# A graph layer and a parallel LSTM on one core: additions moved from GpSimd to VectorE, the state comparison moved three steps ahead, stores on two queues, zeros and the fc weight in other shapes

## Chip, core and metric

The kernel runs on one core of a Trainium2 chip. The metric is the device time of one execution in microseconds (us); the kernel before takes 1112.99 us, the median of three runs (1111.95, 1112.99 and 1113.43). A core has five instruction queues, each in order: TensorE (PE; PEld are its weight loads), VectorE (DVE), ScalarE (ACT), GpSimd (POOL) and SyncE (SP). SP, ACT and POOL also issue DMA transfers.

## The reference, cut to what matters

```python
x = x + gnn(layernorm(x), src, dst, ...)       # 1250 nodes of 512 features, 20000 edges
x = x + lstm(layernorm(x))                     # one sequence of 1250 steps, hidden size 512

def gnn(feat, src, dst, ...):
    h = feat @ fc_w.T + fc_b
    norm = clip(segment_sum(1, dst), 1) ** -0.5
    res = layer(h, h, w1_1, w2_1, b_1, 1)
    return layer(res, h, w1_2, w2_2, b_2, 2)   # layer: sum over edges, two 512x512 products, bias, relu

def step(h_prev, c_prev, x_t):                 # combined = [x_t, h_prev]
    f, i, o = (sigmoid(combined @ W + b) for W, b in three gates)
    c = f * c_prev + i * tanh(combined @ W_c + b_c)
    h = o * tanh(c)                            # h is the output of the step
```

## The kernel before

**Rows.** The 1250 rows are cut into 32 stretches (`P`) of 40 rows (`LEN`). A tile of 128 partitions holds four rows of each stretch, and ten tiles (`T`) hold all rows.

**Start.** In the block that opens the pools `prep`, `edges` and `psT`, SP and ACT issue the loads in the order of the code: edge lists (L292), the last rows of x (L134, on ACT), tile 0 of x (L120), the weight `fcw` as one transfer of 1 MB (L300), tiles 1 to 3 (L120), the bias `fcb`, tiles 4 to 9 (L126), then `w2`, two biases and the zeros. There are eight counters for the transfers of SP and ACT, used in turn: a transfer that takes a counter again waits until the transfer eight places before it has landed. GpSimd makes `ident`, the numbers `ids_f` and a block of zeros in `planes` (L320, 12 partitions of 6144 elements), which SP writes to ten DRAM tensors (L322).

VectorE turns the edge lists into numbers of tiles and stretches (`neg_floor_div`), takes the layer norm's statistics of the tiles (`stats`, `scales`), and compares for the one-hot matrices (`make_onehot`, L401 and L403). TensorE transposes `fcw` (`turn_fcw`, L377: for each of four blocks of columns, four transposes of 128x128), multiplies the tiles (`product`, L176) and adds up the adjacency counts (`count_group`, L417). The order in which PE, DVE and ACT take this work is the order of the code, written by hand in the loop over `s`, for `T + 3` slots.

**Middle.** After two graph layers (L750) the input part of the gates is multiplied for the LSTM (L919) and written to the DRAM tensors `xp_d`, from which each step fetches its 96 rows.

**LSTM.** The 32 stretches run side by side, 40 steps (n = 0 to 39) after 96 steps of warm-up from zero state: 12 in a short form, 84 as full steps (n = -84 to -1). A step is a chain in two halves `s`: matmuls with the state (L604, `add_gates`), three activations (L611, L613, L615), product and sum (L617, L618), tanh (L620), the output `hh` (L621) and its transpose `hT` (L622), which the next step's matmuls wait for. From n = 0 on, GpSimd adds `hh` to the row buffer `x2c` (L1032); after n = 7, 15, 23, 31, 37 and 39 the finished rows are stored (`store`, L831). All stores are issued by SP but the last, which goes over SP, ACT and POOL.

**Comparison.** The warm-up is right where a stretch's state at n = 0 is the state that the stretch before it has after its step 39. `keep_state` (L890, L891) copies states at n = 0 and after the loop; then four DVE instructions (L1039 to L1043), a matmul (L1045) and a conversion (L1047) count the places that are further apart than `TOL` = 2^-18. Every engine loads this count (L1048); if it is above zero, all 1250 steps are run again in order (L1050 ff.), else the branch goes to the end of the program (L1110), where all engines meet.

Of the kernel before, what the change touches and what calls it, by code (L numbers as in the profile page):

```python
# [38 lines left out]
def gnn_lstm_kernel(  # L39
# [118 lines left out]
        nc.vector.tensor_scalar(ve, mv[:, :, 1], EPS, None, OP.add)  # L158
        rsqrt(pool, ve, out, name)

    def transpose_in(ps, rows):

        p = ps.tile([128, KD, R], F32, name="psT")
        for k in range(KD):
            nc.tensor.transpose(p[:, k, :], rows[:, k * 128:(k + 1) * 128], ident)
        return p
# [37 lines left out]
    with ExitStack() as gnn_stack:  # L204
# [77 lines left out]
        with tc.tile_pool(name="prep", bufs=1) as prep, \  # L282
# [14 lines left out]
            load_last_rows(xt, nc.scalar, fill=True)  # L297
            load_rows(0, 1, xt)
            fcw = prep.tile([128, KD, D], F32, name="fcw")
            nc.sync.dma_start(fcw, fc_w.rearrange("(a p) i -> p a i", p=128))  # L300
            biases = [prep.tile([R, D], F32, name=name) for name in ("fcb", "b1", "b2")]
            fcb, *bl = biases
            load_rows(1, 4, xt)
# [12 lines left out]
            nc.gpsimd.iota(ids_f, pattern=[[1, widest]], base=0, channel_multiplier=0,  # L316
                           allow_small_or_imprecise_dtypes=True)

            zeros = planes.rearrange("b t i d -> b (t i d)")[:4 * EARLY, :12 * G]
            nc.gpsimd.memset(zeros, 0.0)  # L320
            for v in xp_d:
                nc.sync.dma_start(  # L322
                    bass.AP(tensor=v.tensor, offset=v.offset,
                            ap=[[12 * G, 4 * EARLY], [1, 12 * G]]), zeros)

            with tc.manual_schedule(engines={mybir.EngineType.PE, mybir.EngineType.DVE,
                                             mybir.EngineType.Activation}):
# [9 lines left out]
                def scales(t0, t1):  # L337
                    layernorm_scale(prep, mv[:, t0:t1, :], rstd[:, t0:t1], f"ln{t0}")
                    nc.vector.scalar_tensor_tensor(nmr[:, t0:t1], mv[:, t0:t1, 0], -1.0,
                                                   rstd[:, t0:t1], op0=OP.mult, op1=OP.mult)  # L340


                ends = []
                for name, rows in rows_i:
# [7 lines left out]
                    nc.vector.tensor_copy(e, p[:ER, 0:2, :EC // 2])  # L352
                    ends.append(e.rearrange("p i c -> p (i c)"))
                e_src, e_dst = ends
                none = edges.tile([ER, BW * T], F16, name="none")
                nc.vector.memset(none, 0.0)
                ids = edges.tile([ER, widest], F16, name="ids")
# [14 lines left out]
                fcT = prep.tile([128, KD, D], F32, name="fcT")  # L372

                def turn_fcw(k):
                    p = psM.tile([128, D], F32, name="psM")
                    for a in range(KD):
                        nc.tensor.transpose(p[:, a * 128:(a + 1) * 128],  # L377
                                            fcw[:, a, k * 128:(k + 1) * 128], ident)
                    nc.scalar.copy(fcT[:, k, :], p)

                turn_fcw(0)
                turn_fcw(1)
                np_src, o_src = neg_floor_div(e_src, LEN, "stretch")
                stats(0, 1)
                scales(0, 1)
                turn_fcw(2)
                na_src, q_src = neg_floor_div(o_src, 4, "tile")
                nc.vector.scalar_tensor_tensor(low, np_src, -4.0, q_src, op0=OP.mult, op1=OP.add)
                nc.vector.scalar_tensor_tensor(key, e_dst, float(T), na_src,
# [31 lines left out]
                            done.append((blocks.pop(i), i))  # L421
                    return done

                xns, xTs, hTs, ps_h, ps_b = {}, {}, {}, {}, {}

                def normed(t):
                    if t < T:
                        xns[t] = work.tile([R, D], F32, name="xn")
                        nc.scalar.activation(xns[t], xt[:, t, :], AF.Identity,
                                             bias=nmr[:, t:t + 1], scale=rstd[:, t:t + 1])  # L430

                BATCH = 4
                n_batch = EC // BATCH
                counted = 0
# [30 lines left out]
                for s in range(T + 3):  # L465
                    c0, c1, c2 = per_slot[s] if s < len(per_slot) else (0, 0, 0)
                    if 0 < s < 3:

                        ps_h[s - 1] = product(psM, xTs.pop(s - 1), fcT)
                        count(c0)  # L470
                    if s < T:
# [12 lines left out]
                    count(c1)  # L484
                    if 0 <= s - 2 < T:
                        hTs[s - 2] = transposed(prep2, psT, h[:, s - 2, :], "hT")
                    if 0 <= s - 1 < T:
                        nc.vector.tensor_add(h[:, s - 1, :], ps_h.pop(s - 1), fcb)
                    count(c2)
                    if s == 2:  # L490
                        for l in range(2):
                            with_identity(w2[l], ALPHA * betas[l], ALPHA * (1.0 - betas[l]))
                    if 0 <= s - 3 < T:


                        hT = hTs.pop(s - 3)
                        ps, name = (psM, "psM") if s < T + 1 else (acc, "acc")
                        if s == T + 1:
                            total(psT.tile([128, KD, R], F32, name="psT")[:1, 0, :1])
                            split_first(prep2, order[3:7])  # L500
                        if s == T + 2:
                            add_base(T - 2)
                            split_first(prep2, order[7:9])
                        ps_b[s - 3] = [product(ps, hT, w2[0], name)]
                        if s == T:
                            most_edges()
                            count_edges(psT.tile([128, KD, R], F32, name="psT")[:, 0, :])
# [351 lines left out]
        def lstm(first_yT, Wx, bx, Wh, wh_parts, close_wx):  # L859
# [4 lines left out]

            TOL = 2.0 ** -18
# [7 lines left out]
            with ExitStack() as pools:  # L875
# [8 lines left out]
                held = S.rearrange("b i r -> b (i r)")[:, :3 * 256].rearrange(  # L884
                    "b (n x y) -> b n x y", n=3, x=8)
                snap, last, apart = held[:, 0], held[:, 1], held[:, 2, :, :31]

                def keep_state(dst, hT):
                    for s in range(2):
# [86 lines left out]
                with tc.manual_schedule(engines={mybir.EngineType.PE, mybir.EngineType.DVE,  # L976
# [32 lines left out]
                    fetch_wanted()  # L1009
                    for n in range(-WARM, LEN):  # L1010
                        u = AHEAD + WARM + n
                        if n == 0:
                            keep_state(snap, hT)
                        if u == len(units):
                            load_x2c()
                        xs = steps.pop(0)
# [11 lines left out]
                            cell(cells, ps[s], cgs[s], s, hh, hT[s])  # L1028
                        if u < len(units):
                            put(u, 2)  # L1030
                        if n >= 0:
                            nc.gpsimd.tensor_add(x2c[:, n, :], x2c[:, n, :], hh)  # L1032
# [7 lines left out]
                nc.vector.scalar_tensor_tensor(apart, apart, -1.0, apart, op0=OP.mult, op1=OP.max)  # L1040
                nc.vector.tensor_scalar(apart, apart, TOL, None, OP.is_le)
                near = seq.tile([128, 1], F32, name="near")
                nc.vector.tensor_reduce(near, apart, mybir.AxisListType.XY, OP.add)  # L1043
                pc = ps_c.tile([R, G], F32, name="pc")[:1, :1]
                nc.tensor.matmul(pc, near, ones, start=True, stop=True)  # L1045
                far = seq.tile([1, 1], I32, name="far")
                nc.vector.tensor_scalar(far, pc, -1.0, float(128 * 8 * 31), OP.mult, OP.add)  # L1047
# [67 lines left out]
```

## Time and profile before

| | us |
|---|---|
| Median of three runs | 1112.99 |
| The profiled execution | 1113.26 |
| Its span, first to last instruction | 1111.5 |
| Start, before TensorE is filled | 0 to 36 |
| Rest of the edge counting and first products | 36 to 195 |
| Graph layers, gate inputs, short warm-up | 195 to 485 |
| Full warm-up steps, n = -84 to -1 | 485 to about 918 |
| Steps n = 0 to 39 | to 1100.6 |
| After the last step | 1100.6 to 1111.5 |

In a timeline a row gives the start, the duration, the engine, the line of the code, the operation, output and inputs, and in brackets how long the engine stood idle before the row and what ended that. A queue's name with a q (POOLq, SPq) marks work of the sequencer alone, such as a DMA issue, a branch or a drain; it is not counted as busy. Tiles that were placed in another's memory show that one's name: `adj` in the LSTM is `sg`, `pr`, `th` or `hh`, `S` holds the kept states, `base` is x at the start and `x2c` in the LSTM.

### The profile page before, as it was taken

Reading aid. Unit: us, or ns where it says so; the run is one execution under the profiler, and the core shown is the slowest. Engines: PE = TensorE matmul, PEld = TensorE weight load, DVE = VectorE, ACT = ScalarE, POOL = GpSimd, SP = SyncE. Lnnn points to the kernel's source line nnn. Section 1 sums busy time; section 2 is a strip of 40 time slices with the busy share of each in tenths; the row PEclk is TensorE's granted clock in tenths of the full one; section 3 lists DMA queues with packets and bytes.
Section 4 is the critical chain, followed back from the end, with each engine's and each line's share of the span. In section 5 each row is a group of like instructions: output and inputs, shape, how many; then the busy total and the mean of one; then the engine's idle time right before and its main releaser. Section 6 shows DMA issues by size and latency. Waiting matters only on the chain.

```text
span 1111.5 us, 26611 instructions
## 1 busy us (share of the span) xinstructions
PE 1007.0 (91%) x10972; PEld 517.7 (47%) x10972; DVE 516.4 (46%) x1753; ACT 342.8 (31%) x1267; POOL 81.9 (7%) x138
## 2 busy tenths in 40 slices
PE   4899999999999998999999988888888888888884
PEld 2455454554455443344444444444444444444442
DVE  7767667102400665655544544444444444444443
ACT  2322125203401024443333333333333333333332
POOL 2000000100000011111001170000000000011001
PEclk9899999999999999999999999999999999999998
DMA  7500000600200037662323393332233333334431
GB/s 217 79 1 1 1 1 35 234 1 18 74 1 1 0 113 230 205 184 82 109 85 114 101 231 97 97 90 87 88 89 99 88 88 87 107 77 116 119 78 20
DMA packets 37271, 98.51 MB, mean 89 GB/s; under 512 B 5711, under 2 KB 10680, under 8 KB 37018
## 3 DMA queue, kind: packets, MB, share of 16 engines
q1 hardware_dynamic: 27280, 68.67, 23.1%
q0 software_dynamic: 7232, 23.63, 6.2%
q10 hardware_dynamic: 2625, 4.39, 1.3%
q8 instruction: 89, 1.46, 0.5%
q14 instruction: 45, 0.36, 0.1%
HBM read 74.29 MB, written 19.76 MB: 85 GB/s over the span
## 4 chain that ended last, share of the span: by engine, by line
PE 49%; issue 26%; DVE 13%; ACT 7%; DMA 1%; SPq 1%; POOL 1%; DVEq 0%; ACTq 0%; POOLq 0%
PE gates L604 29%; PE psM L919 8%; PE psM L176 8%; DVE adj L617 3%; ACT adj L620 3%; DVE hT L622 2%; DVE cg L618 2%; DVE adj L621 2%; ACT cg L611 2%; PE acc L417 2%; ACT adj L613 2%; DVE od L403 1%; DMA fcw<-in_L_gnn_fc_w_dram 1%; POOL xp_d L939 1%; PE gates L596 1%
## 5 line engine op out<-in xcount | busy, mean ns | idle before, releaser
L604 PE MATMUL gates<-Wh,hT 128*32 128x256 f32 x7936 | 457.5, 381 | 61.4 <-DVE hT L622 61.3
L604 PEld LDWEIGHTS gates<-Wh,hT 128*32 128x32 f32 x7936 | 233.4, 109 | 257.1 <-DVE hT L622 122.9
L617 DVE TENSOR_TENSOR adj<-adj,cg 128x128 f32<-128x128 f32 x248 | 68.2, 275 | 231.7 <-ACT adj L613 231.5
L919 PE MATMUL psM<-Wx,xT 128*128 128x512 f32 x320 | 147.6, 607 | 0.5 <-DVE adj L929 0.5
L750 PE MATMUL agg<-adj,planes 128*128 128x512 bf16 x720 | 130.1, 344 | 1.9 <-DVE x L463 1.9
L611 ACT ACTIVATE cg<-gates 128x64 f32<-128x64 f32 x248 | 55.4, 224 | 213.6 <-PE gates L604 210.1
L620 ACT ACTIVATE adj<-cg 128x64 f32<-128x64 f32 x248 | 63.6, 256 | 131.7 <-DVE cg L618 131.7
L750 PEld LDWEIGHTS <-planes 128*128 128x128 bf16 x720 | 70.4, 98 | 62.4 <-DVE x L463 2.7
L621 DVE TENSOR_TENSOR adj<-adj 128x64 f32<-128x64 f32 x248 | 55.9, 225 | 82.5 <-ACT adj L620 82.5
L919 PEld LDWEIGHTS psM<-Wx,xT 128*128 128x128 f32 x320 | 58.7, 192 | 71.3 <-issue 69.0
L622 DVE STREAM_TRANSPOSE hT<-adj 128x64 f32<-128x64 f32 x248 | 60.9, 245 | 24.2 <-DVE adj L621 1.4
L613 ACT ACTIVATE adj<-gates 128x128 f32<-128x128 f32 x248 | 67.2, 271 | 0.1
L618 DVE TENSOR_TENSOR cg<-adj 128x64 f32<-128x64 f32 x248 | 55.8, 225 | 8.5
L939 POOL DMA_DIRECT2D xp_d<-planes x40 | 28.8, 719 | 408.4 <-issue 214.2
L176 PE MATMUL psM<-w,hT 128*128 128x512 f32 x128 | 58.6, 610 | 0.0
L615 ACT ACTIVATE adj<-gates 128x64 f32<-128x64 f32 x248 | 57.0, 230 | 0.0
L403 DVE TENSOR_SCALAR od<-ids,key 125x820 f16<-125x820 f16 (+42 forms) x160 | 55.6, 347 | 0.0
L596 PE MATMUL gates<-h,sel 96*32 96x256 bf16 x992 | 50.0, 273 | 0.0
L1032 POOL TENSOR_TENSOR base<-base,adj 128x128 f32<-128x128 f32 x40 | 18.4, 459 | 414.9 <-DVE adj L621 414.9
L417 PE MATMUL acc<-od,ob 125*128 125x400 f16 (+22 forms) x360 | 46.4, 259 | 0.4
L401 DVE TENSOR_SCALAR ob<-ids,low 125x128 f16<-125x128 f16 x160 | 39.6, 247 | 15.5 <-PE acc L417 15.4
L931 ACT CAST planes<-adj 128x512 bf16<-128x512 f32 x40 | 24.7, 618 | 60.8 <-DVE adj L929 60.7
(163 smaller groups left out, 722.3 us busy)
## 6 DMA issues: line engine op xcount, KB each, us to landing
h<-xp_d SPq DMA_DIRECT2D x136, 384.0 KB
xp_d<-planes POOLq DMA_DIRECT2D x40, 384.0 KB, 3.1
base<-x POOLq DMA_DIRECT2D x40, 64.0 KB, 4.5
w<-in_L_gnn_w_dram SPq DMA_DIRECT2D x2, 1024.0 KB
w<-in_L_gnn_w_dram POOLq DMA_DIRECT2D x2, 1024.0 KB, 5.9
xp_d<-planes SPq DMA_DIRECT2D x10, 144.0 KB
h<-in_x_dram SPq DMA_DIRECT2D x10, 128.0 KB
h<-in_x_dram SPq DMA_DIRECT2D x10, 120.0 KB
```

Of the source, the lines that this page charges most:

```text
L176: nc.tensor.matmul(p, lT[:, k, :], rhs[:, k, :], start=(k == 0), stop=(k == KD - 1))
L417: nc.tensor.matmul(blocks[i][:, (d0 - i * BW) * T:(d1 - i * BW) * T], ob, od[:, (d0 - lo) * T:(d1 - lo) * T], start=False, stop=last)
L604: nc.tensor.matmul(ps[s][32 * j:32 * (j + 1), :, :], hT[b // 2][:, b % 2, :], Wh[:, b, :, 128 * j + 64 * s:128 * j + 64 * (s + 1)], start= ...
L611: nc.scalar.activation(cg[:, 1, :], p[:, 3, :], AF.Tanh)
L613: nc.scalar.activation(sg, p[:, 0:2, :], AF.Sigmoid)
L617: nc.vector.tensor_mul(pr, sg, cg)
L618: nc.vector.tensor_add(cg[:, 0, :], pr[:, 0, :], pr[:, 1, :])
L620: nc.scalar.activation(th, cg[:, 0, :], AF.Tanh)
L621: nc.vector.tensor_mul(hh[:, m], so, th)
L622: nc.vector.transpose(hT.rearrange("p b c -> p (b c)"), hh[:, m])
L750: nc.tensor.matmul(p[:, :n * R], planes[:, k, pl, f * 128:(f + 1) * 128], adj[:, k, t0:t0 + n, :].rearrange("b i r -> b (i r)"), start=(k ...
L919: nc.tensor.matmul(p, yT[n][:, k, :], quarter(Wx[:, k, :, :], j), start=(k == 0), stop=(k == KD - 1))
```

## The change

It has five parts: the addition of `hh` goes from GpSimd to VectorE; the two states are kept at n = -3 and n = 37 (`CHECK` = 3) and compared inside the loop, with the count taken behind the work of step 37; the last store is issued by SP and ACT, four transfers each; the zeros are 96 rows of 768 elements in place of 12 of 6144; `fcw` is loaded in four transfers and turned block by block, each block as it stands in memory, and the statistics of tile 0 come ahead of the arithmetic on the edges.

```diff
+    def transpose_in(ps, rows, name="psT"):
+        p = ps.tile([128, KD, R], F32, name=name)
...
-            nc.sync.dma_start(fcw, fc_w.rearrange("(a p) i -> p a i", p=128))
+            for a in range(KD):
+                nc.sync.dma_start(fcw[:, a, :], fc_w[a * 128:(a + 1) * 128, :])
...
-            zeros = planes.rearrange("b t i d -> b (t i d)")[:4 * EARLY, :12 * G]
+            W = 768
+            zeros = planes.rearrange("b t i d -> b (t i d)")[:4 * EARLY * 12 * G // W, :W]
             nc.gpsimd.memset(zeros, 0.0)
...
+                def turn_fcw(a):
+                    p = transpose_in(psM, fcw[:, a, :], "psM")
+                    nc.scalar.copy(fcT[:, :, a * 128:(a + 1) * 128], p)
...
                 e_src, e_dst = ends
+                stats(0, 1)
+                scales(0, 1)
+                turn_fcw(0)
+                normed(0)
+                turn_fcw(1)
+                xTs[0] = transposed(work, psT, xns.pop(0), "xT")
                 none = edges.tile([ER, BW * T], F16, name="none")
...
-                turn_fcw(0)
-                turn_fcw(1)
                 np_src, o_src = neg_floor_div(e_src, LEN, "stretch")
-                stats(0, 1)
-                scales(0, 1)
-                turn_fcw(2)
...
-                normed(0)
                 onehots(0)
                 onehots(1)
+                turn_fcw(2)
                 turn_fcw(3)
...
-                (nc.sync, nc.scalar, nc.gpsimd, nc.sync)[j if n1 == LEN else 0].dma_start(
+                (nc.scalar if n1 == LEN and j % 2 else nc.sync).dma_start(
...
+                def compare():
+                    nc.vector.tensor_sub(apart, last[:, :, 0:31], snap[:, :, 1:32])
+                    nc.vector.scalar_tensor_tensor(apart, apart, -1.0, apart,
+                                                   op0=OP.mult, op1=OP.max)
+                    nc.vector.tensor_scalar(apart, apart, TOL, None, OP.is_le)
+                    nc.vector.tensor_reduce(near, apart, mybir.AxisListType.XY, OP.add)
+                def count_apart():
+                    pc = ps_c.tile([R, G], F32, name="pc")[:1, :1]
+                    nc.tensor.matmul(pc, near, ones, start=True, stop=True)
+                    nc.vector.tensor_scalar(far, pc, -1.0, float(128 * 8 * 31), OP.mult, OP.add)
...
-                        if n == 0:
+                        if n == -CHECK:
                             keep_state(snap, hT)
+                        if n == LEN - CHECK:
+                            keep_state(last, hT)
+                            compare()
...
+                        if n == LEN - CHECK:
+                            count_apart()
                         if n >= 0:
-                            nc.gpsimd.tensor_add(x2c[:, n, :], x2c[:, n, :], hh)
+                            nc.vector.tensor_add(x2c[:, n, :], x2c[:, n, :], hh)
...
-                    keep_state(last, hT)
-                nc.vector.tensor_sub(apart, last[:, :, 0:31], snap[:, :, 1:32])
...
                 n_far = nc.values_load(far, min_val=0, max_val=128 * 8 * 31)
```

More of the change, by code (lines that the diff above doesn't have):

```diff
@@ L159, in layernorm_scale @@
         rsqrt(pool, ve, out, name)
-    def transpose_in(ps, rows):
-        p = ps.tile([128, KD, R], F32, name="psT")
+    def transpose_in(ps, rows, name="psT"):
+        p = ps.tile([128, KD, R], F32, name=name)
         for k in range(KD):
@@ L323, in gnn_lstm_kernel @@
                     bass.AP(tensor=v.tensor, offset=v.offset,
-                            ap=[[12 * G, 4 * EARLY], [1, 12 * G]]), zeros)
+                            ap=[[W, 4 * EARLY * 12 * G // W], [1, W]]), zeros)
             with tc.manual_schedule(engines={mybir.EngineType.PE, mybir.EngineType.DVE,
@@ L340, in scales, with normed @@
                                                    rstd[:, t0:t1], op0=OP.mult, op1=OP.mult)
+                xns, xTs, hTs, ps_h, ps_b = {}, {}, {}, {}, {}
+                def normed(t):
+                    if t < T:
+                        xns[t] = work.tile([R, D], F32, name="xn")
+                        nc.scalar.activation(xns[t], xt[:, t, :], AF.Identity,
+                                             bias=nmr[:, t:t + 1], scale=rstd[:, t:t + 1])
+                fcT = prep.tile([128, KD, D], F32, name="fcT")
+                def turn_fcw(a):
+                    p = transpose_in(psM, fcw[:, a, :], "psM")
+                    nc.scalar.copy(fcT[:, :, a * 128:(a + 1) * 128], p)
                 ends = []
@@ L370, in neg_floor_div @@
                     return q, r
[L372 to L379, printed above, removed]
-                turn_fcw(0)
-                turn_fcw(1)
                 np_src, o_src = neg_floor_div(e_src, LEN, "stretch")
-                stats(0, 1)
-                scales(0, 1)
-                turn_fcw(2)
                 na_src, q_src = neg_floor_div(o_src, 4, "tile")
@@ L422, in count_group @@
                     return done
[L424 to L430, printed above, removed]
                 BATCH = 4
@@ L470, in gnn_lstm_kernel @@
                         count(c0)
-                    if s < T:
+                    if 0 < s < T:
                         xTs[s] = transposed(work, psT, xns.pop(s), "xT")
@@ L859, in lstm @@
         def lstm(first_yT, Wx, bx, Wh, wh_parts, close_wx):
-            TOL = 2.0 ** -18
+            TOL, CHECK = 2.0 ** -18, 3
             first = -(WARM + BEFORE) % LEN // 4
@@ L886, in lstm @@
                 snap, last, apart = held[:, 0], held[:, 1], held[:, 2, :, :31]
+                near = seq.tile([128, 1], F32, name="near")
+                far = seq.tile([1, 1], I32, name="far")
+                def compare():
[8 more added lines that the diff above has]
+                    nc.vector.tensor_scalar(far, pc, -1.0, float(128 * 8 * 31), OP.mult, OP.add)
                 def keep_state(dst, hT):
@@ L1030, in lstm @@
                             put(u, 2)
+                        if n == LEN - CHECK:
+                            count_apart()
                         if n >= 0:
-                            nc.gpsimd.tensor_add(x2c[:, n, :], x2c[:, n, :], hh)
+                            nc.vector.tensor_add(x2c[:, n, :], x2c[:, n, :], hh)
                             if n + 1 in stores:
                                 store(x2c, ([0] + stores)[stores.index(n + 1)], n + 1)
-                    keep_state(last, hT)
-                nc.vector.tensor_sub(apart, last[:, :, 0:31], snap[:, :, 1:32])
[L1040 to L1047, printed above, removed]
                 n_far = nc.values_load(far, min_val=0, max_val=128 * 8 * 31)
```

## The prediction

> **What bounds the kernel now.** I read the page first, then one step before and one after n = 0, then the end, then the start. The page's costliest group shows what most of the span is:
>
> ```profile
> L604 PE MATMUL gates<-Wh,hT 128*32 128x256 f32 x7936 | 457.5, 381 | 61.4 <-DVE hT L622 61.3
> ```
>
> A step is a chain through the state; TensorE's only idle time is the wait for `hT`. What isn't on that chain costs nothing in the loop. Two steps in the timeline, n = -14 and n = 20 to 21:
>
> ```profile
> 858.48 0.23 DVE L621 TENSOR_TENSOR adj<-adj 128x64 f32<-128x64 f32 x1 [0.32 <-ACT adj L620]
> ```
>
> ```profile
> 1013.53 0.24 DVE L622 STREAM_TRANSPOSE hT<-adj 128x64 f32<-128x64 f32 x1
> ...
> 1015.45 0.29 DVE L617 TENSOR_TENSOR adj<-adj,cg 128x128 f32<-128x128 f32 x1 [1.68 <-ACT adj L613]
> ...
> 1016.39 0.23 DVE L621 TENSOR_TENSOR adj<-adj 128x64 f32<-128x64 f32 x1 [0.39 <-ACT adj L620]
> ```
>
> Read L621's idle time: 0.32 us without GpSimd's addition, 0.39 with it. The instruction records show an extra semaphore wait there: `hh` has three buffers, so from n = 3 on L621 must also wait for GpSimd's reading of three steps ago. From transpose to transpose a step takes 4.46 us before n = 0 and 4.53 from n = 3. VectorE idles 1.68 us after the second transpose.
>
> The end, in the timeline and in the records of line L1110:
>
> ```profile
> 1100.23 0.23 DVE L621 TENSOR_TENSOR adj<-adj 128x64 f32<-128x64 f32 x1 [0.32 <-ACT adj L620]
> 1100.54 0.46 POOL L1032 TENSOR_TENSOR base<-base,adj 128x128 f32<-128x128 f32 x1 [4.09 <-DVE adj L621]
> 1100.56 0.25 DVE L622 STREAM_TRANSPOSE hT<-adj 128x64 f32<-128x64 f32 x1
> ...
> 1102.69 0.41 DVE L1043 TENSOR_REDUCE near<-S 128x1 f32<-128x248 f32 x1
> ...
> 1103.38 0.14 DVE L1047 TENSOR_SCALAR far<-pc 1x1 int32<-1x1 f32 x1 [0.28 <-PE pc L1045]
> ```
>
> ```profile
> L1110 POOLq DRAIN  x3: 46/107/4558, 1106.1 to 1111.2; - x3
> L1110 SPq DRAIN  x3: 7/7/13, 1106.7 to 1110.9; - x3
> ```
>
> The path is comparison (to 1103.52), load of `far`, branch, and GpSimd's own closing: a semaphore update of 1.29 us from 1104.74, then a drain of 4.56 us from 1106.06 to 1110.61. SP was at its drain at 1106.7 and waited 4 us.
>
> The start, in the timeline:
>
> ```profile
> 2.01 5.21 POOL L320 MEMSET planes<- 12x6144 bf16 x1
> ...
> 3.18 4.19 DVE L346 CAST src_f<-src_i 80x250 f32<-80x250 int32 x1 [2.29 <-DMA src_i<-in_src_dram]
> ...
> 8.46 0.28 DVE L346 CAST dst_f<-dst_i 80x250 f32<-80x250 int32 x1
> ...
> 25.17 0.68 DVE L153 BATCH_NORM_STATS2 bnst<-base 128x6 f32<-128x512 f32 x1
> ...
> 36.07 1.12 PE L165 MATMUL psT<-ident,xn 128*128 128x128 f32 x4 [3.39 <-ACT xn L429]
> ```
>
> The same cast takes 4.19 us beside the memset and 0.28 alone; it ends with the memset. VectorE then works nearly without a pause until it lets TensorE start at 36.07; from there to 195 TensorE is 96% busy (153 of 159 us). So what VectorE gains before 36 moves all that follows.
>
> **Part 1, zeros in short rows.** The memset's 5.21 us for 6144 elements a partition make 0.65 for 768, if it goes by elements: done at 2.7, before the cast begins at 3.18. The cast then takes 0.28: 3.91 us off VectorE's chain. Bounds: 0 if GpSimd is no faster, 3.91 if it is out of the way; I take 3.91, since nothing else starts at 3.18. The ten transfers of 96 rows cost SP some 0.6 to 0.9 each (L126's issues of 90 to 96 rows: 0.59 to 0.93), 6 to 9 us against 19.5 now. Nothing but zeros is behind them until SP loads the count of edges at about 184, and `planes` is not overwritten before 171; without that cover they would be on the path for at most 9 us.
>
> **Part 2, fc weight in blocks, tile 0 first.** Sixteen transposes and four copies of 0.59 remain. Tile 0's statistics no longer have their square root behind two `fcT` copies on ACT (13.03 to 13.97): some 0.9 us. VectorE's new chain from the rows: `dst_e` done at 9.87 - 3.91 = 5.96 (tile 0's last piece landed at 4.95); statistics and scale 2.5 us, 8.47; `none` and `ids` 0.65, 9.1; arithmetic 1.6 + 2.15, 12.85; first eight one-hot pairs 2.4, 15.25; tiles 1 to 3 4.2, 19.45; four pairs 1.2, 20.65. That is where L153 stands at 25.17 now: 4.5 us earlier. On ACT and PE the four copies end at about 12.7, when the last block is there at 11.4, against 16.65 now: the product of tile 0 isn't late.
>
> But these statistics (tiles 4 to 6) need all eight transfers of L126, the last of which landed at 23.88 with its issue begun at 19.21. In the new order `fcb` waits for the counter of the last `fcw` block, the statistics of tiles 4 to 6 for what follows it. If that block lands at 11.4 as `fcw` did, `fcb` is issued to 12.0, the eighth of L126 begins 5.37 later (13.84 to 19.21 now) at 17.4, and lands 4.67 later: 22.05. VectorE stands from 20.65 to 22.05, so the gain is 25.17 - 22.05 = 3.1. Bounds: three more issues of 0.51 put the block 1.5 us later, gain 1.6; landing as early as the faster pieces of `fcw` (9.5) frees all 4.5.
>
> A rule speaks against this: the Trainium skill, page "DMA: Bandwidth & Descriptors", section "Measured (HBM→SBUF, 128 partitions, SWDGE, issued from GpSimd)", wants transfers of 1 MiB, and its fixed 2 us per transfer would, as an estimate, put four blocks in a row 6 us later: the start would lose 2.9 and the sum be 1109.7. The trace's row is that the first three transfers behind `fcw` (landed 11.44) landed 0.3 us apart on this queue, at 11.76, 12.09 and 12.41, which is why I don't take it.
>
> TensorE's clock is the start's second unknown: granted 0.88 over 36 to 60, with eight matmuls at 5.49 us in the half-clock stretch (34.8 to 41.6) against 3.66 later. With 5.5 us of work in it, a full clock would gain 2.75, and one more half window of 3.4 us cost 1.7. The gap of 3.39 before 36.07 stays, as its cause (statistics of tiles 7 to 9 ahead of tile 3 on ACT) does: I take no change.
>
> **Part 3, addition on VectorE.** L621 loses GpSimd's wait: 37 steps x 0.07 = 2.6 us. The build's order has the addition right behind the second transpose, so the next matmuls aren't held up. Its price, from L617 (128x128, two inputs, 0.25 to 0.29 us), fits into the idle 1.68. Queued behind it is only L617, for ACT. Hidden: 0; in the path it would be 0.32 x 40 = 12.8.
>
> **Part 4, comparison.** The first copy (four instructions, 0.9 us) moves from n = 0 to n = -3, under the same idle time: 0. At n = 37 the chain from the transpose's start to the end of L1043 is 1103.10 - 1100.56 = 2.54; with 0.27 for the addition 2.81, against 1.92 (1013.53 to 1015.45) that the loop allows: it delays L617 by 0.9, once. The matmul on `near` (0.19) falls into TensorE's wait of 0.6.
>
> **Part 5, end.** `far` is ready two steps (9.1 us) before the last transpose, about 1092. GpSimd, with no step work left, needs 7.06 from load to the end of its drain: 1099, before the last step ends. Then SP decides. Its four issues end as now, 1102.74 (the addition ends at 1101.0 on either engine); load to drain took 1103.55 to 1106.8 = 3.25, so 1102.79 + 3.25 = 1106.0, and the 0.84 from the meeting to the end gives 1106.9 against 1111.45: 4.55 gained. ACT's four issues (now two in 1.11) end near 1103.3 and land 1.6 later, when SP comes to their counters: 0 to 0.3. If the drain of 4.56 isn't hidden, nothing of it is gained.
>
> **Sum.** 3.1 + 2.6 - 0.9 + 4.5 = 9.3 off the profiled execution's 1113.26 gives 1104.0; that execution lies 0.27 above the median, so 1103.7.
>
> **Rivals.** (a) *The start gives nothing*: the rows of x or a half-clock window take back the 3.1. For it: L153 at 25.17 began only 1.3 us after its last input landed. 1106.8, with a half window more 1108.5. (b) *The drain stays last*: its length may belong to closing after the branch, whenever the others come; no other row of the trace has such a drain (0.19 at the start). 1103.7 + 4.5 = 1108.2. (c) *Slower: the addition gets into the state's path*, ahead of the transpose or holding L617: at 0.32 in each of 40 steps 12.8 more, 1103.7 + 12.8 = 1116.5. It decides from 9.3 / 40 = 0.23 us per step on, where the gain is used up. For it: two inputs and 128 columns make it longer than the 0.17 by which the transpose is overlapped with what follows. The build's order and the idle 1.68 us speak against it. (d) *The comparison fails three steps earlier* and all 1250 steps follow in order: at 4.46 us each, 5.6 ms more. Recomputed from the reference's inputs in double precision, the states differ by at most 0.87e-6 at n = -3, tolerance 3.8e-6.
>
> **How the numbers follow.** The forecast 62%, its own range 1100.5 to 1106.5 (start 4.5 and a full clock; start 1.6 and some tenths); (a) 20%; (b) 12%; (c) 3%; (d) 1%; the rest is (a) and (b) together at 1111.3. The range 1099.5 to 1109 takes in (a) and (b) alone and leaves out some 15%. A measurement tells about 0.2%, 2.2 us, from no change: faster 0.91, within 0.05, slower 0.04.
>
> **What would show it.** The cast near 0.3 us; L153 of tile 4 near 22; TensorE filled near 33; steps of 4.46 from n = 0; one step of 5.4 at n = 37; GpSimd's drain ended before SP's, and the end some 6.4 us after the last L621. I am wrong if the steps get longer, if the last piece of x still lands at 24, or if the drain begins or ends after the last store.

## The result and the profile after

| | before | after |
|---|---|---|
| Median, us | 1112.53 (4 runs, 1111.95 to 1113.43) | 1103.20 (4 runs, 1100.89 to 1103.53) |
| Ratio, 95% interval | | 0.9911 (0.9894 to 0.9928) |
| Profiled execution, span | 1113.26, 1111.5 | 1103.53, 1101.7 |
| Second transpose of step n = -84 | 487.43 | 484.21 |
| The same of n = -1 | 918.29 | 915.39 |
| The same of n = 39 | 1100.56 | 1095.73 |
| From there to the end of the span | 10.9 | 6.0 |

The change saves 9.3 us in the medians and 9.7 in the profiled spans: 2.9 up to n = -1, 1.9 in the 40 steps, 4.9 behind them.

First the start, in the timeline of the kernel after (start, duration, engine, line, operation, and in brackets the idle time before it with what ended it):

```profile
2.00 0.73 POOL L323 MEMSET planes<- 96x768 bf16 x1
3.00 0.29 DVE L364 CAST src_f<-src_i 80x250 f32<-80x250 int32 x1 [2.11 <-DMA src_i<-in_src_dram]
...
21.78 0.69 DVE L153 BATCH_NORM_STATS2 bnst<-base 128x6 f32<-128x512 f32 x1 [1.47 <-issue]
...
32.70 1.11 PE L165 MATMUL psT<-ident,xn 128*128 128x128 f32 x4 [3.39 <-ACT xn L350]
```

The zeros are done before the cast begins, and the cast takes 0.29 us. VectorE comes to the statistics of tile 4 at 20.3 and stands for 1.47. The timeline names no cause ("issue"), but by the semaphore records the last of the eight L126 transfers landed at 21.60, just before the statistics begin. TensorE's transposes of tile 3 start 3.4 us earlier than before.

One step of the 40 in the same timeline:

```profile
1004.69 0.23 DVE L624 TENSOR_TENSOR adj<-adj 128x64 f32<-128x64 f32 x1 [0.32 <-ACT adj L623]
1005.02 0.24 DVE L625 STREAM_TRANSPOSE hT<-adj 128x64 f32<-128x64 f32 x1
1005.19 0.25 DVE L1058 TENSOR_TENSOR base<-base,adj 128x128 f32<-128x128 f32 x1
...
1006.95 0.29 DVE L620 TENSOR_TENSOR adj<-adj,cg 128x128 f32<-128x128 f32 x1 [1.50 <-ACT adj L616]
```

L624 (L621 before) idles 0.32 in both halves. The addition L1058 stands behind the transpose and 1.50 us of idle time are left behind it.

Step 37, with the comparison:

```profile
1081.81 0.25 DVE L625 STREAM_TRANSPOSE hT<-adj 128x64 f32<-128x64 f32 x1
...
1084.06 0.41 DVE L901 TENSOR_REDUCE near<-S 128x1 f32<-128x248 f32 x1
1084.38 0.28 DVE L620 TENSOR_TENSOR adj<-adj,cg 128x128 f32<-128x128 f32 x1
...
1087.08 0.10 DVE L906 TENSOR_SCALAR far<-pc 1x1 int32<-1x1 f32 x1
```

L620 has no idle time here: VectorE came late. And the end, in the timeline and in the records of the line where the engines meet (duration shortest, median and longest in ns, then the first and last start in us):

```profile
1096.18 1.80 SPq L834 DMA_DIRECT2D out_dram<-base  x4
1096.18 2.07 ACTq L834 DMA_DIRECT2D out_dram<-base  x4
```

```profile
L1123 POOLq DRAIN  x3: 46/107/4391, 1089.5 to 1101.5; - x3
L1123 SPq DRAIN  x3: 7/7/13, 1100.9 to 1101.2; - x3
```

GpSimd's long drain begins at 1089.5 and is over at 1093.9, before the last step. SP's, at 1100.9, is now the last.

### The profile page after: what moved, and what is told of

Its sections match the earlier page's. It is cut to its first block, busy times and chain, and to the rows that moved or that the text cites. A ratio compares the mean times of both kernels' runs of the same rounds, so it can differ in the third digit from the quotient of the medians.

```text
span 1101.7 us, 26574 instructions
## 1 busy us (share of the span) xinstructions
PE 1007.8 (91%) x10956; PEld 518.8 (47%) x10972; DVE 520.2 (47%) x1793; ACT 343.8 (31%) x1267; POOL 57.9 (5%) x96
## 4 chain that ended last, share of the span: by engine, by line
PE 49%; issue 26%; DVE 14%; ACT 7%; DMA 1%; SPq 1%; POOL 1%; DVEq 0%; ACTq 0%; POOLq 0%
PE gates L607 29%; PE psM L939 8%; PE psM L176 8%; DVE adj L620 3%; ACT adj L623 3%; DVE hT L625 2%; DVE adj L624 2%; DVE cg L621 2%; ACT cg L614 2%; PE acc L428 2%; ACT adj L616 2%; DVE od L414 1%; POOL xp_d L959 1%; PE gates L599 1%; DVE ob L412 1%
## 5 line engine op out<-in xcount | busy, mean ns | idle before, releaser
L620 DVE TENSOR_TENSOR adj<-adj,cg 128x128 f32<-128x128 f32 x248 | 68.3, 276 | 222.9 <-ACT adj L616 222.5
L753 PE MATMUL agg<-adj,planes 128*128 128x512 bf16 (+1 forms) x704 | 129.1, 343 | 2.7 <-DVE x L466 1.9
L624 DVE TENSOR_TENSOR adj<-adj 128x64 f32<-128x64 f32 x248 | 56.0, 226 | 80.4 <-ACT adj L623 80.4
L621 DVE TENSOR_TENSOR cg<-adj 128x64 f32<-128x64 f32 x248 | 55.8, 225 | 8.5
L176 PE MATMUL psM<-w,hT 128*128 128x512 f32 x128 | 56.9, 596 | 0.0
L599 PEld LDWEIGHTS <-sel 96*32 96x32 bf16 x992 | 26.6, 97 | 34.8 <-issue 15.9
```

Of the source, the lines that this page charges most:

```text
L176: nc.tensor.matmul(p, lT[:, k, :], rhs[:, k, :], start=(k == 0), stop=(k == KD - 1))
L599: nc.tensor.matmul(ps[s][32 * j:32 * (j + 1), :, :], lhs(j), rhs(j, s), start=True, stop=False)
L620: nc.vector.tensor_mul(pr, sg, cg)
L621: nc.vector.tensor_add(cg[:, 0, :], pr[:, 0, :], pr[:, 1, :])
L624: nc.vector.tensor_mul(hh[:, m], so, th)
L753: nc.tensor.matmul(p[:, :n * R], planes[:, k, pl, f * 128:(f + 1) * 128], adj[:, k, t0:t0 + n, :].rearrange("b i r -> b (i r)"), start=(k ...
```

## The experiments

All edits are to the kernel after. Their ratios are to the kernel before, from runs beside them; it measured 1112.3 to 1114.2 (medians) in the four groups of runs. A single trace is split at three marks, the second transposes of n = -84, n = -1 and n = 39. Six traces that share the changed start (the kernel after, `u3`, `u4`, `u5`, `c1`, `c2`) reach n = -84 at 483.7 to 485.1, mean 484.4, so a difference there counts from about 0.7 us on. The intervals of two ratios together leave some 0.0022, 2.5 us, open, and those of `u1` to `u4` overlap that of the kernel after. But every run of `u1` to `u5` and `c1` (1104.0 to 1108.5) is above every run of the kernel after (1100.9 to 1103.5), with the kernel before at 1112.3 to 1112.7 beside all of them.

| Kernel | us (median) | ratio, 95% | n = -84 at | 40 steps | behind them |
|---|---|---|---|---|---|
| before, profiled | 1112.5 | 1 | 487.4 | 182.3 | 10.9 |
| after | 1103.2 | 0.9911 (0.9894 to 0.9928) | 484.2 | 180.3 | 6.0 |
| `u1_long_zeros` | 1105.1 | 0.9934 (0.9920 to 0.9948) | 486.0 | 180.0 | 6.2 |
| `u2_one_fcw` | 1105.5 | 0.9934 (0.9921 to 0.9947) | 486.1 | 180.0 | 6.2 |
| `u3_add_on_gpsimd` | 1105.9 | 0.9939 (0.9925 to 0.9954) | 484.9 | 182.5 | 7.6 |
| `u4_compare_at_end` | 1106.9 | 0.9936 (0.9921 to 0.9951) | 485.1 | 179.5 | 10.5 |
| `u5_three_queues` | 1106.7 | 0.9957 (0.9944 to 0.9971) | 483.7 | 180.0 | 10.5 |
| `c1_add_first` | 1107.1 | 0.9952 (0.9937 to 0.9968) | 484.5 | 184.7 | 5.5 |
| `c2_spread` | 1103.1 | 0.9904 (0.9889 to 0.9918) | 484.0 | 179.7 | 6.2 |
| `b1_fcb_later` | 1102.0 | 0.9916 (0.9902 to 0.9929) | 481.8 | 180.0 | 6.0 |
| `w1_warm_pe` | 1103.9 | 0.9915 (0.9901 to 0.9929) | 483.7 | 180.1 | 6.3 |
| `w3_stats_later` | 1100.4 | 0.9893 (0.9878 to 0.9908) | 482.3 | 179.7 | 6.3 |
| `x1_stats_spread` | 1104.9 | 0.9931 (0.9906 to 0.9955) | 484.0 | 179.5 | 6.4 |
| `x2_three_parts` | 1098.7 | 0.9872 (0.9854 to 0.9891) | 479.7 | 179.2 | 6.3 |

**Zeros in long rows again.**

```diff
-            W = 768
+            W = 12 * G
```

> The changed kernel with the zeros filled as before, in 12 rows of 6,144 elements; the rest as changed. Theory: the 5.2 us fill holds VectorE's port again, the cast of src_f takes about 4.2 us instead of 0.29 and VectorE reaches the statistics of tile 4 at about 24.2 instead of 20.3; of these 3.9 us the 1.47 that it now waits for rows of x are given back, so 2.4 us are lost at the start and the time is about 1105.6. Rival: the four blocks of the fc weight made the gain of the start and the cast has room to spare, so the time stays at 1103.2.

Its timeline:

```profile
3.19 4.17 DVE L364 CAST src_f<-src_i 80x250 f32<-80x250 int32 x1 [2.31 <-DMA src_i<-in_src_dram]
...
24.30 0.68 DVE L153 BATCH_NORM_STATS2 bnst<-base 128x6 f32<-128x512 f32 x1
```

The cast is slow again, tile 4's statistics come 2.5 us later and without a wait, as the theory said. TensorE's transposes of tile 3 start at 35.21, also 2.5 later, but step -84 only 1.6 later than the mean. The ratio is up by 0.0023, 2.6 us. So the short zeros are worth some 1.6 to 2.6 us, and the rival falls.

The cast runs from 3.19 to 7.36 and the fill to 7.21, so VectorE ends with GpSimd here as it did before the change. The Trainium skill, page "SBUF — State Buffer", section "Who interferes with whom", has it so: GpSimd and a VectorE cast can want the same pair of ports, and whoever is second is blocked until the first has finished. The rows agree: 4.17 us beside the fill, 0.29 after it.

**The fc weight in one transfer.**

```diff
-            for a in range(KD):
-                nc.sync.dma_start(fcw[:, a, :], fc_w[a * 128:(a + 1) * 128, :])
+            nc.sync.dma_start(fcw, fc_w.rearrange("(a p) i -> p a i", p=128))
```

> The changed kernel with the fc weight loaded in one transfer of 1 MB; zeros as short rows, order of the turning as changed. Theory: its last byte lands at about 11.4 instead of 9.8, what SP issues behind it comes about 1.6 us later, so the statistics of tile 4 begin at about 23.4 and the time is 1104.8. Rival (a large transfer moves faster than four small ones, as the Trainium skill's page DMA: Bandwidth & Descriptors, section Measured (HBM->SBUF, 128 partitions, SWDGE, issued from GpSimd), has it for its own setup): the rows of x come no later or earlier, and the time is 1103.2 or up to 1 us less.

Its timeline:

```profile
11.13 1.97 PE L165 MATMUL psM<-ident,fcw 128*128 128x128 f32 x8 [5.58 <-DMA fcw<-in_L_gnn_fc_w_dram]
12.89 0.55 SPq L304 DMA_DIRECT2D fcb<-in_L_gnn_fc_b_dram  x1
...
23.75 0.69 DVE L153 BATCH_NORM_STATS2 bnst<-base 128x6 f32<-128x512 f32 x1 [1.36 <-DMA base<-in_x_dram]
```

TensorE gets the weight at 11.13, where the four blocks had landed at 6.27, 6.90, 8.61 and 9.82 by the semaphore records of the kernel after. SP issues `fcb` at 12.89 in place of 10.41, and tile 4 waits until 23.75 in place of 21.78. Step -84 is 1.7 later than the mean, the ratio 0.0023 higher. The theory holds. The rule of the Trainium skill that the prediction weighed (page "DMA: Bandwidth & Descriptors", section "Measured (HBM→SBUF, 128 partitions, SWDGE, issued from GpSimd)") doesn't hold for this queue: four transfers of 256 KB had all landed by 9.82, the one of 1 MB at 11.09. Why the last block is earlier too was not tried.

**The addition on GpSimd.**

```diff
-                            nc.vector.tensor_add(x2c[:, n, :], x2c[:, n, :], hh)
+                            nc.gpsimd.tensor_add(x2c[:, n, :], x2c[:, n, :], hh)
```

> The changed kernel with the addition of x2c and the state on GpSimd again; comparison and stores as changed. Theory: a step is 0.07 us longer again (4.53 instead of 4.46), 2.6 us over 37 steps, and GpSimd's closing, some 7 us from its last instruction, starts behind the last addition and ends about 2.4 us after SP's: together some 5 us, 1108. Rival 1: the end is set by SP whatever GpSimd does, so only the 2.6 us of the steps come back (1105.8). Rival 2: the wait in the step was not the addition's, the steps stay at 4.46 and only the end is lost (1105.6).

One row of a step in its timeline, and its records of the meeting:

```profile
1013.53 0.22 DVE L624 TENSOR_TENSOR adj<-adj 128x64 f32<-128x64 f32 x1 [0.39 <-ACT adj L623]
```

```profile
L1123 POOLq DRAIN  x3: 46/107/4395, 1100.4 to 1105.3; - x3
L1123 SPq DRAIN  x3: 7/7/13, 1103.1 to 1105.0; - x3
```

The 0.39 is back, and the steps are 4.526 us instead of 4.46 from n = 3 on: 182.5 for 40, against a mean of 180.0 in the seven traces with the addition behind the transpose on VectorE and the whole comparison in step 37. That is 2.5 us. GpSimd's reading of three steps ago was long over when L624 came to it: what costs 0.07 is the second wait, which the instruction records show as a semaphore instruction of its own ahead of the first half's L624. GpSimd's drain begins at 1100.4, 2.0 us behind its last addition, and ends at 1104.8, while SP was there at 1103.1: 1.6 us at the end. Both terms of the theory are there, the second smaller than 2.4, since GpSimd loaded `far` and branched beside its last addition (the load begins at 1097.91, the addition at 1097.95). The ratio is up by 0.0028, 3.1 us; the trace's parts give 4.1.

**The comparison behind the last step.** The two `keep_state`, `compare` and `count_apart` go back to n = 0 and behind the loop.

> The changed kernel with the states kept at step 0 and after step 39 and the comparison behind the last step, as before the change; addition on VectorE, last rows on two queues. Theory: far is ready some 3 us after the last step instead of 13 us ahead of the end, GpSimd's closing of 7 us follows it and ends the program again: about 4.9 us lost, against 0.5 us won because no comparison stands in step 37: 1107.6. Rival: the drain of SP and ACT behind the last landing takes as long as GpSimd's closing now that these queues carry the stores, so no more than 1 us is lost (1103.2 to 1104.2).

Its records of the meeting:

```profile
L1121 POOLq DRAIN  x3: 46/107/4395, 1100.7 to 1105.7; - x3
L1121 SPq DRAIN  x3: 7/7/13, 1101.3 to 1105.4; - x3
```

SP waits 4 us for a drain of 4.4, as before the change; 10.5 us lie behind the last transpose in place of 6.0 to 6.4. Steps 37 to 39 take 4.48 each and the 40 steps 179.5: the comparison in step 37 cost 0.5. The runs spread over 1104.0 to 1107.8 (ratio up by 0.0025, 2.8 us), and the profiled one was the slowest. The sizes are from its trace: 4.3 lost at the end, 0.5 won. The rival falls.

**The last rows over three queues.**

```diff
-                (nc.scalar if n1 == LEN and j % 2 else nc.sync).dma_start(
+                (nc.sync, nc.scalar, nc.gpsimd, nc.sync)[j if n1 == LEN else 0].dma_start(
```

> The changed kernel with the last two rows stored over SP, ScalarE, GpSimd and SP as before; addition and comparison as changed. Theory: GpSimd issues its transfers until about 1098 and its closing of some 5.9 us (a semaphore update and a drain of 4.4) follows, so it ends the program some 3 us after SP would: about 1106. Rival: two queues and three take the same time, SP decides the end with either, 1103.2; on its own side, the GpSimd issues could even shorten SP's row of issues by 0.5 us.

Its timeline and its records of the meeting:

```profile
1095.06 1.10 POOL L834 DMA_DIRECT2D out_dram<-base  x2 [430.01 <-DVE base L1058]
```

```profile
L1123 POOLq DRAIN  x3: 46/107/4554, 1099.5 to 1104.6; - x3
L1123 SPq DRAIN  x3: 7/7/13, 1100.0 to 1104.3; - x3
```

Theory. GpSimd issues two transfers to 1096.2, waits 1.5 for their landing, updates the semaphores for 1.29 and drains for 4.55, to 1104.0 (1.29 and 4.56 before the change, 1.25 and 4.39 in the traces without stores on GpSimd); SP was there at 1100.0. 10.5 us lie behind the steps, 4.3 more than in `u1` and `u2`; the ratio is up by 0.0046, 5.1 us. The expected 3 left out the wait for the landing. So the end needs both parts of the change: an early `far` and no store on GpSimd. Either alone gains 0.4 of the 4.9 us there.

**The addition ahead of the transpose.**

```diff
             nc.vector.tensor_mul(hh[:, m], so, th)
+            if first:
+                first()
             nc.vector.transpose(hT.rearrange("p b c -> p (b c)"), hh[:, m])
```

`first` is the addition, in the second half of the steps from n = 0 on; it is taken out of its place behind the halves.

> The changed kernel with each step's addition on VectorE ahead of the second transpose of the state instead of behind it, so that it lies on the way of the state. Theory: an addition of 0.25 to 0.29 us that now lies in VectorE's idle 1.7 us would cost its whole length in each of the 40 steps, 10 to 12.8 us: 1113 to 1116, which is the price of the slower rival and shows that behind the transpose it costs nothing. Rival: the transpose waits 0.32 us for its multiplication anyway, or the second half has slack of its own, so it costs less than 0.1 a step, under 4 us.

Its timeline:

```profile
1002.11 0.23 DVE L624 TENSOR_TENSOR adj<-adj 128x64 f32<-128x64 f32 x1 [0.32 <-ACT adj L623]
1002.37 0.29 DVE L1054 TENSOR_TENSOR base<-base,adj 128x128 f32<-128x128 f32 x1
1002.57 0.24 DVE L627 STREAM_TRANSPOSE hT<-adj 128x64 f32<-128x64 f32 x1
```

Neither theory nor rival has the size: a step takes 4.586 in place of 4.46, 0.13 more, and 40 steps 184.7 in place of 180.0. Behind L624 the transpose of its result starts after 0.33 us; with the addition between them it starts after 0.46. The instruction records show the parts. Without the addition the transpose waits for L624 and for TensorE, and the wait for L624 is a semaphore instruction of its own. In this run the addition, which needs L624's result too, takes that wait and starts 0.26 behind L624; the transpose has one wait left and starts 0.20 behind the addition, before the addition's 0.29 have passed. The place behind the transpose is still worth 4.7 us in the 40 steps (0.5 to 0.7 come back at the end, where the last rows are ready earlier; ratio 0.0041, 4.6 us).

**The comparison in two parts.** The copies and the subtraction stay at n = 37; the rest goes ahead of step 38, the count behind it.

> The changed kernel with the comparison in two parts: the copies and the subtraction ahead of step 37, the absolute value, the test and the sum ahead of step 38, each part short enough for VectorE's idle 1.5 us. Theory: step 37's extra 0.5 us go, step 38 stays at 4.46, far is ready one step later (about 1091) and GpSimd's closing still ends ahead of SP's: 1102.7. Rival: the extra time was the rhythm of the steps and not the comparison (other steps have 0.35 more now and then), so the time stays 1103.2; or the closing comes to lie on the end again, which would cost up to 1 us.

The first L620 of step 38 in its timeline:

```profile
1087.97 0.29 DVE L620 TENSOR_TENSOR adj<-adj,cg 128x128 f32<-128x128 f32 x1 [0.43 <-ACT adj L616]
```

The idle 0.43 shows that VectorE has time left. Steps 37 and 38 take 4.49 each, steps 37 to 39 together 13.33 in place of 13.92 in the kernel after. The 40 steps are only 0.3 below the usual 180.0, since most steps of this trace are 0.005 longer than in the others. In the runs this is below what they can tell (1103.1 and 1103.2; ratio 0.0007 lower).

**Warm transposes in TensorE's idle time.** 16 transposes of `ident` into `acc`, read by nobody, stand ahead of `transposed` at slot 3.

> The changed kernel with 16 transposes of the identity on TensorE, some 2.6 us at full clock, just ahead of the transposes of tile 3's rows, whose results are read by nobody. Theory: TensorE's idle 3.4 us at 29.3 are filled, the stretch of 6.8 us at half clock behind them goes, and up to 3.4 us are won although the rows come no earlier: 1100 to 1101; then the clock is at least half of what putting the statistics off had won. Rival: the half clock behind the idle time is hidden by VectorE and the time stays within 0.5 of 1103.2, or the extra transposes hold up the real ones and it is up to 1.5 us longer; then the gain of the later statistics was the wait itself.

Two windows of 4 us, of the kernel after, then of this one (after the window and its length: busy us of PE, PEld, DVE, ACT and POOL with the number of instructions, the granted clock, the DMA share and GB/s):

```profile
32.00:36.00 4.00, 3.17 (x10) 2.02 (x11) 3.83 (x22) 4.00 (x4) 0.00 (x0) 0.55 0.01 4
36.00:40.00 4.00, 4.00 (x7) 1.61 (x6) 3.32 (x18) 1.91 (x3) 0.00 (x0) 0.59 0.00 0
```

```profile
32.00:36.00 4.00, 3.14 (x11) 1.63 (x12) 3.86 (x23) 4.00 (x4) 0.00 (x0) 0.87 0.02 4
36.00:40.00 4.00, 4.00 (x17) 1.82 (x16) 3.36 (x19) 1.62 (x3) 0.00 (x0) 0.71 0.00 0
```

The clock behind the filled time is higher, one half-clock stretch of 3.4 us in place of one of 6.8, but it doesn't go to full. Step -84 is at 483.7, within the spread, and the ratio is 0.9915 against 0.9911: nothing is won that can be measured. The program doesn't set these stretches alone: in the six traces with the same start the one around 30 to 37 us begins between 28.2 and 33.3 and lasts 3.4, 6.8 or 10.2 us.

The Trainium skill, page "TensorE: Matmul & The Clock Gate", section "Part 1: The HAM clock gate (the "warmup" mystery)", speaks of a free-running window of some 3.4 us. The half-clock stretches of the kernel after, 18.76 to 25.59 and 32.42 to 39.24, agree: each is two windows long.

**Later statistics of tiles 7 to 9.**

```diff
-                    if s < 3:
-                        t0, t1 = ((1, 4), (4, 7), (7, T))[s]
+                    if s in (0, 1, 4):
+                        t0, t1 = {0: (1, 4), 1: (4, 7), 4: (7, T)}[s]
```

> The changed kernel with the statistics and scales of tiles 7 to 9 made at slot 4 of the first stage instead of slot 2, so that the normalised rows of tile 3 no longer stand behind them on ScalarE. Theory: TensorE waits 3.4 us for these rows at 29.3 in the profile of the changed kernel and then runs 6.8 us at half clock; without the wait its transposes begin near 29.5, the half-clock stretch behind them goes or gets shorter, and what is won is 2 to 5 us: 1098 to 1101. Rival: VectorE is what this stage is short of, the work put off returns as a wait of the same length some slots later, and the time stays within 1 us of 1103.2.

The transposes of tile 3 in its timeline, where the kernel after has them at 32.70 behind 3.39 us of waiting:

```profile
28.92 0.63 PE L165 MATMUL psT<-ident,xn 128*128 128x128 f32 x4
```

The wait is gone, and between 20 and 44 us the granted clock is 1.00 throughout. Step -84 is 2.1 earlier than the mean, the ratio 0.0018 lower (2.0 us). Between 18 and 60 us both this run and the one with warm transposes had one half-clock stretch of 3.4 us, and that one reached step -84 1.4 later. This speaks for the wait, not the clock, as the larger part; with one trace each, and 1.4 between traces of the same start, it isn't shown.

**`fcb` behind the rows of tiles 4 to 9.** The line of `fcb`'s transfer moves below `load_rows(4, T, xt)`.

> The changed kernel with the transfer of fcb issued behind those of the rows of tiles 4 to 9 instead of ahead of them. Theory: the last of these rows lands some 0.6 us earlier, the 1.47 us that the statistics of tile 4 wait shrink to about 0.9, and the time is 1102.6. Rival: fcb then lands after it is needed by the first addition of h, or the start's end is set by the clock windows, and the time is 1103.2 or more.

The statistics of tile 4 start at 20.40 without a wait, 1.4 earlier, and step -84 is at 481.8, 2.6 before the mean. But the profiled run was the fastest of its five (1100.3; median 1102.0), and the ratio, 0.9916, is that of the kernel after. Alone it is inconclusive.

**Statistics at slots 0, 2 and 4, comparison in two parts.** The statistics also go behind `normed(s + 1)` of their slot.

> The changed kernel with the statistics of tiles 4 to 6 at slot 2 and of tiles 7 to 9 at slot 4, both behind the normalised rows of the slot, and the comparison in two parts as in the run beside it. Theory: the wait of 1.1 to 1.5 us for the rows of tile 4 goes too, because they have landed by then; against the run with tiles 7 to 9 alone put off (1100.4) some 1 us more and 0.5 for the comparison: about 1099. Rival: VectorE is busy without a gap from 30 to 40 us in that run, so the statistics moved there push everything behind them by what they save ahead, and only the 0.5 are won: 1100.

A matmul of the adjacency counts in its timeline:

```profile
31.09 1.27 PE L428 MATMUL acc<-od,ob 125*128 125x120 f16 x4 [3.18 <-DVE od L414]
```

A miss, and neither the theory nor the rival's 1100: in the timeline TensorE now waits 3.18 us for one-hot matrices that VectorE makes behind the moved statistics. Step -84 is at 484.0, as in the kernel after, and the runs spread over 1102.7 to 1113.5.

**Three edits together:** the statistics of tiles 7 to 9 at slot 4, `fcb` behind the rows, the comparison in two parts.

> The changed kernel with three edits that were run alone before: the statistics of tiles 7 to 9 at slot 4, fcb issued behind the rows of tiles 4 to 9, the comparison in two parts. Theory: the first takes 2.1 us (step -84 at 482.3 in its trace against a mean of 484.4 in the eight traces with the same beginning), the second 0.6 to 1.5, because VectorE still waits 1.1 for the rows in the first one's trace, the third 0.3 to 0.6 of the 40 steps: 1099 to 1100 beside 1112.5 before, a ratio of 0.988. Rival: the first and the second take the same idle time of TensorE, so together they give what the first gives alone, 1100.4 or a ratio of 0.9893.

(The text says eight traces; 484.4 is the mean of the six named above.) In its timeline:

```profile
20.31 0.68 DVE L153 BATCH_NORM_STATS2 bnst<-base 128x6 f32<-128x512 f32 x1
...
29.80 0.65 PE L165 MATMUL psT<-ident,xn 128*128 128x128 f32 x4 [0.31 <-ACT xn L350]
```

Tile 4's rows are there at 20.31 and tile 3's transposes wait 0.31. Step -84 is at 479.7, 4.7 before the mean, as much as the first two edits give alone in their traces (2.1 and 2.6). The 40 steps take 179.2, 0.9 below the usual; 0.35 of that is one longer step fewer, as in the two other runs with tiles 7 to 9 at slot 4, and its cause is not known. The ratio is 0.9872 (0.9854 to 0.9891), just below the interval of the kernel after: this version is the fastest. The trace speaks against the rival, that the first two edits take the same idle time: it allows 2.1 at n = -84, not 4.7. The ratios don't decide it, since the rival's 0.9893 with 0.3 to 0.6 us for the comparison comes to 0.9888 to 0.9890.

## Why the prediction was right, and where not

**The start, 3.1 forecast.** Measured 3.2 in the two traces, 3.0 against the mean of six. The cast went from 4.19 to 0.29 as worked out, and VectorE then waited for rows of x, which landed at 21.60 (22.05 forecast). That agreement is partly luck: the last block of `fcw` landed at 9.82 and not at 11.4, so the eighth L126 transfer began at 16.39 and not at 17.4, but it landed 5.2 later and not 4.67. The prediction took 23.88 in the trace of before for the last landing; the last of the eight was at 24.46. Nor did `fcb` wait for the last block's counter, as the prediction had it: SP stood for the third block (landed 8.61, issue at 8.62) and then issued without a pause, `fcb` at 10.41. `u1` and `u2` show that both edits share the gain about evenly (1.6 and 1.7 in the traces): either alone, with the new order of tile 0, gave about half. Not all that VectorE gains before 36 us arrives later, as the prediction assumed: in `u1` 2.5 us at tile 3's transposes are 1.6 at n = -84. The clock, the second unknown, did not make the gain: between 17 and 60 us TensorE had 10.2 us of half clock before and 13.7 after.

**The addition, 2.6 forecast.** 2.5 by `u3`, from L624's 0.07 in each step. The cause, a second wait on L621 for GpSimd's counter, is shown by putting the addition back.

**The comparison, 0.9 forecast; mis-sized.** It cost 0.5 (`u4`). The prediction set a chain of 2.81 against 1.92 allowed. Measured from the transpose, L620 begins at 2.57 in step 37 and at 1.95 in the step before: 0.62 late. The chain itself was 2.66 long and not 2.81, since the four copies took 0.61 to the subtraction's start and not 0.73, and L620 begins 0.09 before L901 has ended. Step 38 is then 0.11 shorter (4.354 against 4.467).

**The end, 4.55 forecast.** 4.9 between the two profiled runs, 4.7 against the usual 6.2. GpSimd's closing is hidden, which `u4` and `u5` show by uncovering it; SP decides. SP's way from its load of `far` to the meeting took 2.9 and not the 3.25 of the forecast. Rival (b), that the drain stays last whenever the others come, is refuted: it ran from 1089.5 to 1093.9, with steps still going on.

**The rest.** In the profiled run the steps from n = -64 to -1 were each some 0.005 us longer than before (median 4.463 against 4.458; 282.01 against 281.66 for that stretch, 281.4 to 281.5 in most other traces), which takes 0.35 from the start's gain. The cause is not known. Forecast 9.3 for the sum, measured 9.3 in the medians. So close an agreement is luck: the ratio's interval is 1.9 us to each side, and the smaller price of the comparison and the larger gain at the end stand against the slower steps.

**Rival (c), mis-sized.** Its price of 0.32 in each step was wrong: an addition in the state's path costs 0.13 (`c1`), some 5 us in all, so this misplacement would not have made the kernel slower than before. The prediction took the addition's whole length; part of it overlaps with the transpose, and the addition takes over a wait.

## What to carry to other kernels

At the end of a program each engine's closing work is a chain of its own: give the engine whose closing is longest its last instruction early, its value loads and DMA issues included, and check all of them, since two late transfers on it lost nearly the whole gain here (4.3 of some 4.7 us in `u5`). An instruction moved into a loop belongs behind the last one of the chain that carries the state, where the next wait covers it. Once a start has been shortened, look for the next wait at the same place: here later statistics, a later bias and the comparison in two parts together gave another 0.0039 of the time, 4.3 us.

## What the runs showed of the hardware

- GpSimd's closing is there in all 14 traces: 1.29 us of semaphore update and 4.55 to 4.56 of drain where it had issued transfers shortly before (before, `u5`), 1.25 and 4.39 to 4.40 in the twelve others, also where it had stood idle for over 400 us. The other engines' drains took 7 to 17 ns.
- A VectorE instruction of the step that waits for L624 alone started 0.26 us after it (the addition in `c1`), one that waits for L624 and for another engine 0.33 (the transpose in the kernel after): the second wait is an instruction of its own and cost 0.07, as at L621 before the change (0.39 in place of 0.32). An addition of 0.29 put between L624 and the transpose cost 0.13.
- Four transfers of 256 KB on SP's queue landed by 9.82, one of 1 MB let TensorE begin at 11.13.
- The same start ended at 483.7 to 485.1 in six traces, with stretches of half clock at different places. The same first product (L176, eight matmuls) took 3.70 us from 12.59 in the kernel after and 6.40 from 12.77 in `c1`, where the record of full clock begins at 11.94 and 18.23. Differences below a microsecond in the first stage can't be read from one trace.
